# A hand-written order of TensorE's work in two attentions, written out as a string

## The chip, the core and the metric

The kernel runs on one core of one Trainium2 chip. The metric is the time of one execution on the device in microseconds; three runs of the kernel before gave 2184.05, 2185.17 and 2186.51 us, a median of 2185.17 us. The engines of the core work side by side and each takes its own instructions in order: TensorE (PE in the profile; its weight loads are PEld), VectorE (DVE), ScalarE (ACT), GpSimd (POOL), and SyncE (SP), which issues transfers.

## What is computed

The program is a stack of eight blocks on an input of 2 x 512 rows of 512 numbers in fp32: four attentions, each followed by a feed-forward block, each with a layer norm before it and a residual sum after it. The change touches the first attention and the last one. Both have 32 heads and short head vectors:

```python
def L0_attn_a(x, ...):                       # first attention; 4 numbers per head
    C_q = x @ Wq_d + bq_d
    C_kv = x @ Wkv_d + bkv_d
    q = (C_q @ W_qk + b_qk).reshape(b, s, NUM_HEADS, KV_LAT)
    scores = einsum('bqhd,bkd->bhqk', q, C_kv) / sqrt(KV_LAT)
    attn = softmax(scores, axis=-1)          # no mask
    V = (C_kv @ Wv_u + bv_u).reshape(b, s, NUM_HEADS, HEAD_DIM)
    return einsum('bhqk,bkhd->bqhd', attn, V).reshape(b, s, -1) @ Wo + bo

def L1_attn_b(hidden_states, ...):           # last attention; 16 numbers per head
    q, k, v = split(hidden_states @ qkv_w + qkv_b, 3, axis=-1)
    q, k = _rope(q, cos, sin), _rope(k, cos, sin)
    scores = einsum('bqhd,bkhd->bhqk', q, k) * scale
    scores = scores + (1.0 - causal) * MASK_VAL
    probs = softmax(scores, axis=-1)
    ctx = einsum('bhqk,bkhd->bqhd', probs, v).reshape(b, s, e)
    return ctx @ out_w + out_b
```

The two feed-forward blocks and the two attentions in the middle (`attn_gqa`, `attn_mla`) are not touched.

## The kernel before

The heads are worked in quartets. The four heads of a quartet lie in the four groups of 32 rows (partitions) that TensorE's array can use independently, g = 0 to 3. The first attention (`attn_latent_small`) has 16 quartets in one sequence, 8 for each of the two halves of the batch. The last one (`attn_mha`) runs its function `core` once for each half, with 8 quartets in each. Its `core` is compiled in two versions and a register chooses; the causal one is the one that the profile shows running. There the widths of the products differ: a block of 128 queries sees only the keys up to it, so a product is 128, 256, 384 or 512 wide, while in the first attention all are 512 wide.

A quartet u goes through these steps, each a small function that both attentions define and that a common function orders:

- `score(u, j, g)`: one product on TensorE (S in what follows): the scores of block j of 128 queries, head g, into one bank of PSUM (L474, L1263). VectorE reduces the bank to one maximum per row (L482; L1273, which adds the mask first) and writes it into the tile `nm`. There are 16 of these in a quartet, j = 0 to 3 and g = 0 to 3.
- `maxima(u)`: four transposes on TensorE of `nm` (M; L490, L1287), and on VectorE one addition that puts the negative maxima into a spare row of the queries, the tile `qm` (L492, L1289).
- `transposed(u, j, g)`: one product on TensorE (T) of keys with `qm`, so that the scores come out transposed and with the maximum subtracted (L505, L1299), and its exponential on ScalarE (L508, L1309). There are 16 in a quartet. In the last attention GpSimd clears half a block after each four of them (L1313).
- `values(u)`: 16 products of values with the exponentials, all into one bank (L516, L1324). In the first attention VectorE adds that bank to `raw` (L528; ScalarE copies it for each fourth quartet, L526), in the last one ScalarE copies it (L1332).
- `after`: a list of later steps. `divide` transposes `raw` and divides by the sums (L538 to L546 for each fourth quartet of the first attention, L1338 to L1342 for each quartet of the last). In the first attention `flatten` and `project` follow (L559 to L575). `extra` is a list of 11 pieces of the first attention that prepare the second half of the batch (layer norms, latents, queries, values).

Each step that takes a PSUM bank takes the next of eight in a fixed circle: `turn()` (L131) walks through the list `BANKS` of L127. So a product can start only when the engine that reads the bank taken eight turns before has done so.

TensorE's order is written by hand: `manual_schedule(engines={PE})` (L577, L1349) keeps TensorE's instructions in the order in which the program emits them, while a scheduler places those of the other engines. `run_quartets` (L318) emits them. It is one quartet ahead with the scores: in the pass for u it interleaves the 16 scores of u + 1 with the 16 transposed products of u, block by block: for block 0 four scores and then four transposed products, for the others one and one. After each block there is room for one piece of `extra` or `after`. Then `values(u)` follows, and then `maxima(u + 1)`:

```python
            if 0 <= u < n:
                values(u)
                due.append((u, 0))
            if u + 1 < n:
                maxima(u + 1)
```

So the first pass, u = -1, has nothing but 16 scores and the maxima, and the last one has transposed products and no scores.

Of the kernel before, what the change touches and what calls it, by code (L numbers as in the profile page):

```python
# [37 lines left out]
B, S, D = 2, 512, 512  # L38
P = 128
NT = S // P  # L40
# [5 lines left out]
class Block:  # L46
# [268 lines left out]
                )  # L315

    @staticmethod
    def run_quartets(n, score, maxima, transposed, values, after, extra=()):  # L318

        due, extra = [], list(extra)
        for u in range(-1, n + 1):
            pieces = [due.pop(0)] if due else []
            for j in range(NT):
                for m, (kind, g) in enumerate(
                    ((0, 0), (1, 1), (0, 2), (1, 3), (0, 1), (1, 0), (0, 3), (1, 2))
                    if j
                    else ((0, 0), (0, 1), (0, 2), (0, 3), (1, 0), (1, 1), (1, 2), (1, 3))  # L330
                ):
                    if kind == 0 and u + 1 < n:
                        score(u + 1, j, g)
                    if kind == 1 and 0 <= u < n:
                        transposed(u, j, g)
                if extra and u >= 0:
                    extra.pop(0)()
                elif pieces and j < 3:
                    of, done = pieces[0]
                    if done < len(after):  # L340
                        after[done](of)
                        pieces[0] = (of, done + 1)
            for of, done in pieces:
                for f in after[done:]:
                    f(of)
            if 0 <= u < n:
                values(u)
                due.append((u, 0))
            if u + 1 < n:
                maxima(u + 1)  # L350


def attn_latent_small(k, a):
# [8 lines left out]
    with ExitStack() as ctx:  # L362
# [18 lines left out]
        for i in range(2):  # L381
            m = one([P, NT, P], f"nm{i}")
# [82 lines left out]
        extra = prepare(1) + [fold, fold_bias]  # L465

        quartets = [(b, half, i) for b in range(B) for half in range(2) for i in range(4)]
# [107 lines left out]
                k.add_to_x(b * NT + t, ps)  # L575

        with tc.manual_schedule(engines={mybir.EngineType.PE}):  # L577
            k.run_quartets(
                len(quartets), score, maxima, transposed, values, [divide, flatten, project], extra
            )  # L580


def ffn_lora(k, a):
# [569 lines left out]
def attn_mha(k, a, exact):  # L1153
# [5 lines left out]
    T = 4  # L1159
# [3 lines left out]
    with ExitStack() as ctx:  # L1163
# [26 lines left out]
        for i in range(2):  # L1190
            m = one([P, NT, P], f"nm{i}")
# [50 lines left out]
        def core(b, causal):  # L1242
# [17 lines left out]
            def score(u, qt, g):  # L1260
                kv = (qt + 1) * P if causal else S
                ps = k.turn()
                nc.tensor.matmul(  # L1263
                    ps[:, :kv],
                    q[rows[g], u, bass.ts(qt, P)],
                    kk[rows[g], u, :kv],
                    start=True,
                    stop=True,
                )
                at = 32 * g + spare  # L1270
                lo = S - (qt + 1) * P
                mask = k.mask if causal else add
                nc.vector.tensor_tensor_reduce(  # L1273
                    out=ps[:, :kv],
                    in0=ps[:, :kv],
                    in1=mask[:, lo : lo + kv],
                    op0=ALU.add,
                    op1=ALU.max,
                    scale=1.0,
                    scalar=-3e38,  # L1280
                    accum_out=nm[u % 2][:, qt, at : at + 1],
                )

            def maxima(u):
                tp = k.turn()
                for qt in range(NT):
                    nc.tensor.transpose(tp[:, bass.ts(qt, P)], nm[u % 2][:, qt], k.ident)  # L1287
                t = lp.tile([P, S], F32, tag="qm", name="qm")
                nc.vector.tensor_tensor(t, tp, q[:, u], ALU.add)  # L1289
                qm[u] = t  # L1290

            def transposed(u, kc, g):
                if (u, kc) not in probs:
                    pt = lp.tile([P, 4, S], F32, tag="pT", name="pt") if kc % 2 else k.other()
                    probs[u, kc] = [pt, 0]
                pt = probs[u, kc][0]
                lo = kc * P if causal else 0
                ps = k.turn()
                nc.tensor.matmul(  # L1299
                    ps[:, lo:],  # L1300
                    kk[rows[g], u, bass.ts(kc, P)],
                    qm[u][rows[g], lo:],
                    start=True,
                    stop=True,
                )
                if not causal:
                    at = S - P - kc * P
                    nc.vector.tensor_tensor(ps, ps, addT[:, at : at + S], ALU.add)
                nc.scalar.activation(pt[:, g, lo:], ps[:, lo:], AF.Exp, scale=scale)  # L1309
                probs[u, kc][1] += 1  # L1310
                if causal and probs[u, kc][1] == 4:
                    diag = pt[:, :, lo : lo + P]
                    nc.gpsimd.affine_select(  # L1313
                        out=diag, in_=diag, compare_op=ALU.is_ge, fill=0.0, base=0,
                        pattern=[[0, 4], [1, P]], channel_multiplier=-1,
                    )
# [30 lines left out]
                )  # L1347

            with tc.manual_schedule(engines={mybir.EngineType.PE}):  # L1349
                k.run_quartets(8, score, maxima, transposed, values, [divide])  # L1350
            ctxT = k.other()
            for c in range(T):
                tp = k.turn()
# [11 lines left out]
        for b in range(B):  # L1365
            prepare(b)
            with tc.If(exact != 0) as branch:
                core(b, True)
            with branch.Else():
                core(b, False)  # L1370


@with_exitstack
def kernel(ctx: ExitStack, tc: tile.TileContext, a: dict, out: bass.AP):
    k = Block(ctx, tc, a["x"], out)
    attn_latent_small(k, a)
    ffn_lora(k, a)
    attn_gqa(k, a)
    ffn_lora(k, a)
    attn_mla(k, a)  # L1380
    exact = causal_exact(k, a)
    ffn_moe(k, a)
    attn_mha(k, a, exact)
    ffn_moe(k, a, last=True)
# [157 lines left out]
```

## Time and profile before

| what | us | where it is from |
|---|---|---|
| median of three runs | 2185.17 | the times |
| the profiled execution, its own time | 2187.9 | the times |
| span of the profiled execution | 2186.2 | head of the page |
| TensorE busy in the span | 2083.8 | page, part 1 |
| VectorE busy in the span | 1298.2 | page, part 1 |
| quartets of the first attention, first score reduction to last sum | 260 (28.1 to 288.3) | timeline of VectorE |
| one quartet there, undisturbed | 14.0 to 14.1 | starts of L528 and L492 |
| quartets of the last attention, first half | 100.5 (1851.3 to 1951.8) | timeline of TensorE |
| the same, second half | 99.6 (2009.2 to 2108.8) | timeline of TensorE |
| one quartet there | 11.49 | starts of L1289 |

The time of an execution is 1.7 us above its span: work outside the recorded instructions. The profile writes `out<-in` with the program's names of tiles; `sc`, `pj`, `tp` and `av` are PSUM banks. An fp32 product shows as two matrix multiplications, one pass after the other. Several rows of TensorE overlap where they use different groups of rows, so its "busy" share is not a share of its full speed. In a timeline the bracket at the end of a line is the idle time of that engine ahead of the line and what ended it.

### The profile page before, as it was taken

Reading aid. Unit: us, or ns where it says so; the run is one execution under the profiler, and the core shown is the slowest. Engines: PE = TensorE matmul, PEld = TensorE weight load, DVE = VectorE, ACT = ScalarE, POOL = GpSimd, SP = SyncE. Lnnn points to the kernel's source line nnn. Section 1 sums busy time; section 2 is a strip of 40 time slices with the busy share of each in tenths; the row PEclk is TensorE's granted clock in tenths of the full one; section 3 lists DMA queues with packets and bytes.
Section 4 is the critical chain, followed back from the end, with each engine's and each line's share of the span. In section 5 each row is a group of like instructions: output and inputs, shape, how many; then the busy total and the mean of one; then the engine's idle time right before and its main releaser. Section 6 shows DMA issues by size and latency. Waiting matters only on the chain. (4 is left out here: it accounts for less than half of the span.)

```text
span 2186.2 us, 38883 instructions
## 1 busy us (share of the span) xinstructions
PE 2083.8 (95%) x15128; PEld 1094.9 (50%) x15128; DVE 1298.2 (59%) x3478; ACT 731.3 (33%) x2040; POOL 708.8 (32%) x945
## 2 busy tenths in 40 slices
PE   7999989999999999999998989999999889999988
PEld 3444444555555555555554444454544444554545
DVE  6678842655555555555555556666666584755745
ACT  2555621322222222222222155444544111541531
POOL 1100020423322222232322256555555436115211
PEclk9999989999999999999999999999999999999999
DMA  3000021112121212111010322010101102002001
GB/s 96 15 1 1 20 92 58 49 40 68 25 64 25 64 33 65 37 61 49 21 30 6 119 59 71 2 63 10 58 11 50 39 30 43 1 2 39 1 2 39
DMA packets 65751, 85.35 MB, mean 39 GB/s; under 512 B 13458, under 2 KB 50450, under 8 KB 60948
## 3 DMA queue, kind: packets, MB, share of 16 engines
q1 hardware_dynamic: 64916, 81.70, 12.6%
q8 instruction: 123, 2.02, 0.4%
q10 hardware_dynamic: 640, 1.05, 0.3%
q14 instruction: 72, 0.59, 0.1%
HBM read 58.60 MB, written 2.10 MB: 28 GB/s over the span
## 5 line engine op out<-in xcount | busy, mean ns | idle before, releaser
L239 ACT ACTIVATE room<-room,nmax 128x128 f32<-128x128 f32 (+3 forms) x384 | 211.2, 551 | 505.5 <-DVE nmax L229 504.5
L250 POOL TENSOR_SCALAR room<-room,invs 128x128 f32<-128x128 f32 (+3 forms) x384 | 198.0, 536 | 99.2 <-DVE invs L247 99.2
L677 POOL TENSOR_TENSOR q<-q,t 128x512 f32<-128x512 f32 x64 | 81.9, 1280 | 436.3 <-DVE t L676 436.3
L290 PE MATMUL sc<-turned,vals 32*128 32x128 f32 (+7 forms) x1058 | 190.6, 417 | 0.0
L290 PE MATMUL pj<-turned,vals 32*128 32x256 f32 (+7 forms) x692 | 189.0, 424 | 0.0
L290 PE MATMUL tp<-turned,vals 32*128 32x384 f32 (+7 forms) x676 | 158.8, 430 | 0.0
L218 PE MATMUL sc<-kT,q 128*32 128x256 f32 (+15 forms) x1576 | 145.6, 404 | 11.5 <-DVE invs L247 10.8
L263 DVE STREAM_TRANSPOSE turned<-room 128x1152 f32<-128x1152 f32 x80 | 107.9, 1363 | 73.1 <-POOL room L250 22.2
L290 PEld LDWEIGHTS sc<-turned,vals 32*128 32x128 f32 (+1 forms) x1058 | 126.3, 168 | 8.3 <-issue 5.6
L150 PE MATMUL pj<-room,w 128*128 128x512 f32 x272 | 122.2, 599 | 0.0
L181 POOL TENSOR_TENSOR rstd<-ve,mhalf 128x1 f32<-128x1 f32 x80 | 44.8, 562 | 205.3 <-DVE ve L179 192.4
L290 PEld LDWEIGHTS pj<-turned,vals 32*128 32x128 f32 (+1 forms) x692 | 107.1, 169 | 3.9 <-issue 2.2
L150 PE MATMUL sc<-w,room 128*128 128x512 f32 (+1 forms) x240 | 105.5, 582 | 0.0
L150 PE MATMUL sc<-room,w 128*128 128x512 f32 x232 | 105.2, 596 | 0.0
L290 PE MATMUL av<-turned,vals 32*128 32x256 f32 (+7 forms) x358 | 95.7, 420 | 8.8 <-DVE turned L263 8.8
L150 PE MATMUL sc<-w,ctxT 128*128 128x512 f32 x216 | 100.3, 607 | 2.2 <-ACT ctxT L304 2.2
L218 PE MATMUL tp<-kT,q 128*32 128x288 f32 (+15 forms) x1024 | 93.2, 398 | 2.9 <-POOL q L945 2.0
L290 PEld LDWEIGHTS tp<-turned,vals 32*128 32x128 f32 (+1 forms) x676 | 92.2, 169 | 4.4 <-issue 2.7
L239 ACT ACTIVATE probs<-probs,nmax 128x128 f32<-128x128 f32 (+3 forms) x128 | 71.1, 556 | 67.3 <-DVE nmax L229 66.0
L218 PEld LDWEIGHTS sc<-kT,q 128*32 128x32 f32 x1576 | 63.7, 110 | 58.4 <-issue 17.6
L218 PE MATMUL pj<-kT,q 128*32 128x256 f32 (+4 forms) x992 | 87.4, 386 | 4.9 <-DVE invs L247 4.1
L505 PE MATMUL sc<-qm,keys 32*128 32x512 f32 x200 | 86.8, 637 | 0.8 <-DVE qm L492 0.8
(564 smaller groups left out, 5768.8 us busy)
## 6 DMA issues: line engine op xcount, KB each, us to landing
vals<-v SPq DMA_DIRECT2D x256, 64.0 KB, 2.0
w<-in_b_wq SPq DMA_DIRECT2D x8, 1024.0 KB, 5.3
w<-in_b_wo SPq DMA_DIRECT2D x8, 1024.0 KB, 4.8
w<-in_m_wo SPq DMA_DIRECT2D x8, 1024.0 KB, 6.7
w<-in_f_w SPq DMA_DIRECT2D x4, 1024.0 KB, 4.8
w<-in_m_wqn SPq DMA_DIRECT2D x8, 384.0 KB, 3.1
x<-in_x SPq DMA_DIRECT2D x8, 256.0 KB, 4.6
w<-in_b_wk SPq DMA_DIRECT2D x8, 256.0 KB, 2.8
```

The costliest lines, as they stand in the source:

```text
L150: last = self.nc.tensor.matmul(out, lhsT, rhs, start=(i == 0), stop=(i == len(pairs) - 1))
L181: self.nc.gpsimd.tensor_tensor(r, ve, self.mhalf, ALU.pow)
L218: nc.tensor.matmul(ps[32 * i : 32 * i + 32, a - lo : b - lo], q[:, at : at + 32], keys[:, a:b], start=True, stop=True,)
L239: nc.scalar.activation(row, row, AF.Exp, bias=nmax, scale=-1.0, accum_out=total[:, qt : qt + 1])
L250: self.nc.gpsimd.tensor_scalar(row, row, inv[:, qt : qt + 1], 1.0, ALU.mult, ALU.mult)
L263: self.nc.vector.transpose(out[:, :last], probs[:, :last])
L290: self.nc.tensor.matmul(out[:, :, :n], values(i, j), rhs, start=(j == blocks[0]), stop=(j == stop[i]),)
L505: nc.tensor.matmul(ps, keys[b][rows[g], bass.ts(kc, P)], qm[u][rows[g]], start=True, stop=True)
L677: nc.gpsimd.tensor_tensor(out, out, t2, ALU.add)
```

## The change

`run_quartets` gets two more arguments, `lead` and `order`. The scores are now one list over all quartets. The first `lead` of them are emitted ahead of everything (12 in the first attention, 8 in the last). Then each pass follows a string: S is the next score of the list, whatever its quartet, T the next transposed product of quartet u, M the maxima of u + 1, and a bar a place for one piece of `extra` or `after`. What is left of `after` goes behind the string, and `values(u)` comes last in the pass. The groups of rows are taken in the order 0, 2, 1, 3 by the scores and 1, 3, 0, 2 by the transposed products. With 16 S in each string, a pass begins with 12 (or 8) scores of quartet u + 1 already emitted, and the last 12 (8) of its S belong to quartet u + 2. M stands inside the string, behind the score that completes quartet u + 1, and six S stand at its end, in front of the values.

```diff
-    def run_quartets(n, score, maxima, transposed, values, after, extra=()):
+    def run_quartets(n, lead, order, score, maxima, transposed, values, after, extra=()):
+        scores = iter([(u, j, g) for u in range(n) for j in range(NT) for g in (0, 2, 1, 3)])
         due, extra = [], list(extra)
+        for i in range(lead):
+            score(*next(scores))
         for u in range(-1, n + 1):
-            pieces = [due.pop(0)] if due else []
-            for j in range(NT):
-                for m, (kind, g) in enumerate(
-                    ((0, 0), (1, 1), (0, 2), (1, 3), (0, 1), (1, 0), (0, 3), (1, 2))
-                    if j
-                    else ((0, 0), (0, 1), (0, 2), (0, 3), (1, 0), (1, 1), (1, 2), (1, 3))
-                ):
-                    if kind == 0 and u + 1 < n:
-                        score(u + 1, j, g)
-                    if kind == 1 and 0 <= u < n:
-                        transposed(u, j, g)
-                if extra and u >= 0:
+            left = [(j, g) for j in range(NT) for g in (1, 3, 0, 2)] if 0 <= u < n else []
+            for step in order:
+                if step == "S":
+                    at = next(scores, None)
+                    if at:
+                        score(*at)
+                elif step == "T" and left:
+                    transposed(u, *left.pop(0))
+                elif step == "M" and u + 1 < n:
+                    maxima(u + 1)
+                elif step == "|" and extra and u >= 0:
                     extra.pop(0)()
-                elif pieces and j < 3:
-                    of, done = pieces[0]
-                    if done < len(after):
-                        after[done](of)
-                        pieces[0] = (of, done + 1)
-            for of, done in pieces:
-                for f in after[done:]:
-                    f(of)
+                elif step == "|" and due:
+                    due.pop(0)()
+            for f in due:
+                f()
+            due = []
             if 0 <= u < n:
                 values(u)
-                due.append((u, 0))
-            if u + 1 < n:
-                maxima(u + 1)
+                due = [lambda f=f, u=u: f(u) for f in after]
+        for f in due:
+            f()
...
-            k.run_quartets(
-                len(quartets), score, maxima, transposed, values, [divide, flatten, project], extra
-            )
+            order = "STTST|STSTTSSST|STTTTMTSTSTTT|SSSSSS"
+            steps = score, maxima, transposed, values
+            k.run_quartets(len(quartets), 12, order, *steps, [divide, flatten, project], extra)
...
-                k.run_quartets(8, score, maxima, transposed, values, [divide])
+                order = "STTSTSSTSTTSTSTSTTTTS|TTSTMTSSSSSS"
+                k.run_quartets(8, 8, order, score, maxima, transposed, values, [divide])
```

The numbers of instructions on each engine stay the same. On VectorE and ScalarE the scheduler places them in the order in which TensorE now produces the banks they read.

## The prediction

> **What bounds the kernel now.** I read the page first, then the idle times of the score products by source line, then VectorE's timeline over one undisturbed quartet of each attention, and last TensorE's over the same stretches.
>
> ```profile
> span 2186.2 us, 38883 instructions
> PE 2083.8 (95%) x15128; PEld 1094.9 (50%) x15128; DVE 1298.2 (59%) x3478; ACT 731.3 (33%) x2040; POOL 708.8 (32%) x945
> ```
>
> TensorE looks full, but four products on four groups of rows count as four busy rows at once, so 95% only says that it is seldom empty. What its products wait for is in the answer for line 474 (the scores of the first attention):
>
> ```profile
> its engine sat idle before it (us, times) until:
>   DVE nm L482: 31.0, 98
> ```
>
> 98 times a score stood on its bank until VectorE had reduced the score eight turns before; TensorE's order is fixed, so whatever is behind it stood too. VectorE's timeline of one quartet (start, length, idle ahead in brackets):
>
> ```profile
> 219.14 0.69 DVE L528 TENSOR_TENSOR raw<-tp,raw 128x512 f32<-128x512 f32 x1 [2.43 <-PE tp L516]
> 219.75 0.68 DVE L492 TENSOR_TENSOR qm<-sc,qs 128x512 f32<-128x512 f32 x1
> 220.75 0.69 DVE L482 TENSOR_REDUCE nm<-av 128x1 f32<-128x512 f32 x1 [0.32 <-PE tp L474]
> 221.35 0.68 DVE L482 TENSOR_REDUCE nm<-sc 128x1 f32<-128x512 f32 x1
> ...
> 230.09 0.68 DVE L482 TENSOR_REDUCE nm<-tp 128x1 f32<-128x512 f32 x1
> 233.21 0.69 DVE L528 TENSOR_TENSOR raw<-av,raw 128x512 f32<-128x512 f32 x1 [2.43 <-PE av L516]
> ```
>
> Back to back, VectorE takes 0.60 us for one of these (220.75 to 221.35). A quartet has 18: 10.8 us of 14.07 (219.14 to 233.21). It idles 3.27 us: 2.43 while TensorE does the values, the rest around the maxima and in small gaps. So both engines alternate as the bound: VectorE paces the scores, then starves during the values. The last attention is alike:
>
> ```profile
> 2064.07 0.14 DVE L1273 DVE_READ_ACCUMULATOR2_ANT nm<- 128x1 f32 x1
> 2065.71 0.69 DVE L1289 TENSOR_TENSOR qm<-tp,qs 128x512 f32<-128x512 f32 x1 [1.49 <-PE tp L1287]
> ...
> 2068.22 0.26 DVE L1341 RECIPROCAL inv_all<-sc 128x16 f32<-128x16 f32 x1 [0.81 <-PE sc L1338]
> ```
>
> Its reductions step on by 0.25, 0.38, 0.52 and 0.65 us for 128, 256, 384 and 512 columns, four each: 7.2; the addition 0.62 and the division 0.64 make 8.46 of a period of 11.49.
>
> **What the Trainium skill says.** "TensorE: Matmul & The Clock Gate", Part 3 (Packing small matmuls): products on different row groups run side by side, and products keep program order. The trace agrees on both: four scores start within 0.02 us at 219.59, and all wait behind one that waits. "TensorEngine Tiling (Array Packing)", PSUM Bottleneck: packing speeds TensorE, not the reading of PSUM, which may then bound; here that is the 0.60 per score. The same page, Key Properties: a change of tiling mode drains the array. The trace fits: the values start at 215.43, when the last passes of the products (214.91) have run their 0.43 and some 0.1. "PSUM — Partial Sum Buffer", Terms: eight banks, and one product fills at most one; that is the circle of eight.
>
> **The change, part by part.** No instruction is added or removed and no DMA moves; SP's queue is untouched. GpSimd's clearing instructions keep their order; they were off the path (values waited for them at most some tenths). All cost is in TensorE's order, so I walked one steady quartet of each string by hand. Durations: a 512-wide product holds its row group 0.95 us (two passes of 0.43 and 0.1; 206.49 to 207.43); its bank is readable 1.16 us after its start by VectorE, 1.2 by ScalarE; VectorE 0.60 per score, ScalarE 0.48 per exponential (207.70 to 208.20 and on); M 0.59 (219.00 to 219.59); values 3.57 (215.43 to 219.00).
>
> *First attention, zero at the end of the values.* STTS start at 0 on four row groups, TSTS at 0.95: their banks are those of the last T, of the six scores in front of the values and of the sum, read by then. VectorE does the sum (0.3 to 0.9), idles 0.26, and reduces from 1.16 at full pace. The next products stand on banks: TT at 1.84 (the reduction of the first S, 1.16 to 1.76, frees one), SS at 2.2 and 2.4, STST at 2.7 to 3.6, TTT at 3.7 to 4.2, M when the array has drained, 5.1 to 5.7. Its addition runs 5.96 to 6.56, behind the eighth reduction: no wait is longer for it, since its first user is in the next pass. Then T S T at 5.7 to 6.0; S T T want occupied row groups, 6.65; T S S S at 7.5, S S S at 8.4 to 8.5; drained at 9.4, values to 12.97. VectorE idles 0.3, 0.35 and 0.25 between the thinner scores, finishes the six at 12.3, 0.85 before the next sum. Its idle adds up to 2.0: 10.8 + 2.0 = 12.8 to 13.0. I take 13.0: 1.1 less than 14.07. ScalarE has 7.7 of work and ends its last exponential at 9.3, before the last quarter of the values needs it.
>
> Ramps. Before the first T there are now 28 scores, not 16, so VectorE's additional 12 x 0.60 stand in front; some fill time in which TensorE waited. Following the circle, T's start spreads over 42 to 45 us (39.3 before) and the first values end near 58.5 instead of 55.46, one postponed layer norm allowed for: +2.5 to +3. In exchange the pass before last has 4 scores (about 11.2 us: -2.9), and the last begins with T at once instead of M and its addition (277.30 minus 275.7: -1.6). The 11 extra pieces are TensorE's own work (before, their four long quartets exceed 14.07 by about 26 us with the projection); moved from four to three a pass, I count them at nothing, +-4. Sum: 3 - 13 x 1.1 - 2.9 - 1.6 = -16.
>
> *Last attention.* The same walk with its widths (a product holds its row group 0.95, 0.74, 0.53, 0.32; results arrive 1.16, 0.98, 0.77, 0.55 after the start). The pass begins with the eight wide scores of u + 1; VectorE reduces them from 0.98 to 5.66, waiting 0.37 once; the products in between stand on its banks. The transposes for the division run 5.2 to 5.8 and VectorE's division 5.95 to 6.6; M 6.2 to 6.8, its addition 6.95 to 7.57. The six scores in front of the values are narrow (two 128, four 256 wide), start by 7.1, and cost VectorE 2.0 us, 7.57 to 9.59; values wait for the bank of M, 7.67, and take 2.29 (2074.22 to 2076.51): 9.96. VectorE idles 1.5, 8.46 + 1.5 = 9.96. Taken: 10.0, 1.5 less than 11.49. Ramp: in the first pass the extra scores (two of 128 before the addition) hide under the wait for the maxima, and then VectorE is 2.0 us behind: +0.5. Five steady passes: -7.5. The one before last has eight scores only: -2.4. The last has no M and no wait (1943.98 minus 1942.54): -1.45. Sum -10.9 per half, -22 for two. The projections of the second half (1967.9 to 2009) follow on TensorE without a gap and only move forward.
>
> Total -38. Against the profiled execution, 2187.9 - 38 = 2149.9; it was 2.7 over the median, so 2147 for the median.
>
> **Unknown costs.** The trace shows no stretch of these mixed products without VectorE's pacing for long. If row groups packed ideally, TensorE's share of a quartet would be 8.3 + 3.57 + 0.2 = 12.05: eight rounds of 0.86, one more each for the groups that M and the last S leave unfilled, M, and the values. In the last attention it would be about 9.0 (products 2 x 2.14, values 2.29, two sets of transposes 1.18, drains and occupied groups 1.3, an estimate from the rows above). If each bank came 0.1 later than walked in the five places where the chain passes through one, 13.5 and 10.5. A gain beyond VectorE's 10.8 and 8.46 is excluded, as its work is unchanged. That makes the first attention -9 to -28, the last -16 to -33: ends 2160 and 2124. TensorE's clock is low just after the ramps (passes of 0.84 instead of 0.43 around 1861 to 1868); a longer ramp could keep it low, up to +4 in all.
>
> **Rivals.** (a) Full overlap: VectorE never starves, periods 10.8 and 8.5. Then 13 x 3.27 + 10 x 3.0 + ramps (some 8) is about -80: 2105. For it: six scores are 3.6 us of reductions against 3.57 of values. Against: TensorE's own 12.05. (b) Only one string works, since the other stands on banks as long as before; -16 or -22: 2163 to 2169, and 2174 if the ramp eats more of it. For it: in the first attention eleven T come in the first nineteen steps, and ScalarE's pace holds their banks. (c) Slower: the scores run ahead without shortening a period. The mechanism is head-of-line waiting: six scores in front of the values start only as VectorE frees banks, so they delay the values by up to 6 x 0.60 = 3.6 us, more than the 3.27 of idle that they can fill. It decides from the point where VectorE is still four or more scores behind when the first of the six is due; my walk has it one behind. Then a quartet of the first attention takes 14.4, and with the dearer ramp (+3) the kernel is at +5: 2190. (d) The strings do nothing that counts, because waits only change names: 2185.
>
> **Chances.** Forecast 64% (2135 to 2162), stronger overlap, with (a) at its end, 14% (2095 to 2135), (b) 14% (2162 to 2180), (c) 5%, (d) 3%. Range 2122 to 2167. A measurement of this kernel can tell 0.2%, 4.4 us, from no change: faster 0.92, same 0.03, slower 0.05.
>
> **What would show it.** Right: the starts of L528 and L1289 are 12.2 to 13.5 and 9.6 to 10.5 apart; the idle of VectorE ahead of L528 falls from 2.43 to under 1.2; the first exponential comes near 43 us instead of 42.05; M no longer stands before an idle of the transposed products. Wrong: values that wait for VectorE's banks by more than 1 us, periods above 13.7 or 11.2, or a ramp beyond 5 us.

## The result, and the profile after

The changed kernel takes 2171.97 us (median of 4 runs, 2171.32 to 2172.98), the kernel before, run beside it on the same chip, 2185.84 (2184.05 to 2188.02): a ratio of 0.9937, with a 95% interval of 0.9919 to 0.9954. It is faster by 14 us, where 38 were forecast. The profiled executions differ by 16.5 us of span:

```profile
span 2169.7 us, 38898 instructions
PE 2076.7 (96%) x15128; PEld 1102.2 (51%) x15128; DVE 1298.8 (60%) x3478; ACT 725.5 (33%) x2040; POOL 707.3 (33%) x945
```

The work is the same (VectorE 1298.8 us against 1298.2). What went is waiting. The answer for line 474 of the changed kernel shows that the wait on which the forecast rested fell there:

```profile
its engine sat idle before it (us, times) until:
...
  DVE nm L482: 5.6, 15
```

Before, scores stood on their banks 98 times, 31.0 us in all; now it is 15 times, 5.6 us. But that is one line of four. The same wait ahead of the other products of the first attention fell only from 23.1 to 20.7 us (transposed products 6.8 to 10.8, maxima 6.4 to 9.9, values 9.9 to none). The wait of the transposed products for the addition (L492), 10.0 us before, is gone. The idle time for which the profile shows no releaser ("issue") grew from 53.3 to 67.8 us over the four lines. All idle ahead of them together fell from some 126 to 118 us. These are almost all idle times of the weight loads (PEld), so the measure is rough; but by it most of the waiting that left the scores stands elsewhere now.

The starts of the last step of each quartet tell where the 16.5 us are. In the last attention the last copy of the values (L1332) starts at 2092.3 instead of 2108.9 us and, for the first half, at 1944.5 instead of 1951.9. The sum of the first attention (L528) of the last quartet starts at 291.8 instead of 287.6 us, 4.2 us later, of which 0.2 is a later first reduction. From the first score of a half to its last copy, the last attention takes 89.8 and 90.6 us instead of 100.6 and 99.7: it gained 19.9. The other 0.8 us lies in the blocks between the two attentions, which the change doesn't touch and which took 1560.6 to 1564.0 us over all the runs kept. The loss and the gain are read apart from here on.

**The last attention did what was forecast.** ScalarE's timeline over the second half, its rows for L1332 (start, length, idle ahead in brackets; the exponentials between them are left out):

```profile
2064.76 0.59 ACT L1332 COPY raw<-tp 128x512 f32<-128x512 f32 x1 [2.56 <-PE tp L1324]
...
2074.88 0.59 ACT L1332 COPY raw<-sc 128x512 f32<-128x512 f32 x1 [2.57 <-PE sc L1324]
...
2084.47 0.59 ACT L1332 COPY raw<-sc 128x512 f32<-128x512 f32 x1 [2.04 <-PE sc L1324]
...
2092.32 0.59 ACT L1332 COPY raw<-tp 128x512 f32<-128x512 f32 x1 [1.38 <-PE tp L1324]
```

A steady quartet takes 10.12 us (forecast 10.0, before 11.49), the one before last 9.59, the last 7.85 (before 9.22). In VectorE's timeline of a steady quartet one idle of more than 0.1 us is left, behind the values:

```profile
2035.31 0.57 DVE L1273 CUSTOM_DVE_ANT_0 tp<-tp,mask 128x384 f32<-128x384 f32 x1 [1.45 <-PE sc L1263]
...
2041.25 0.69 DVE L1289 TENSOR_TENSOR qm<-av,qs 128x512 f32<-128x512 f32 x1
...
2043.84 0.14 DVE L1273 DVE_READ_ACCUMULATOR2_ANT nm<- 128x1 f32 x1
2045.43 0.57 DVE L1273 CUSTOM_DVE_ANT_0 sc<-sc,mask 128x384 f32<-128x384 f32 x1 [1.45 <-PE sc L1263]
```

Before, the addition (L1289) stood behind 1.49 us of idle; now VectorE comes to it from other work, and 1.45 us stand ahead of the first score behind the values instead. So the idle at the values is about as long as it was. What went are the idle of 0.81 us ahead of the division, which the prediction's lines show, and one of 0.42 us ahead of a score (L1273 at 2070.52).

**The first attention.** VectorE's timeline of an undisturbed quartet of the changed kernel:

```profile
229.64 0.69 DVE L528 TENSOR_TENSOR raw<-tp,raw 128x512 f32<-128x512 f32 x1 [1.01 <-PE tp L516]
230.66 1.89 DVE L482 TENSOR_REDUCE nm<-sc 128x1 f32<-128x512 f32 x3 [0.33 <-PE sc L474]
...
235.55 0.69 DVE L492 TENSOR_TENSOR qm<-sc,qs 128x512 f32<-128x512 f32 x1
236.64 0.69 DVE L482 TENSOR_REDUCE nm<-sc 128x1 f32<-128x512 f32 x1 [0.40 <-PE sc L474]
237.46 0.69 DVE L482 TENSOR_REDUCE nm<-tp 128x1 f32<-128x512 f32 x1
238.36 0.69 DVE L482 TENSOR_REDUCE nm<-sc 128x1 f32<-128x512 f32 x1 [0.21 <-PE av L474]
...
242.99 0.69 DVE L528 TENSOR_TENSOR raw<-pj,raw 128x512 f32<-128x512 f32 x1 [0.95 <-PE pj L516]
```

It takes 13.35 us (13.39 on the mean of four) where 14.03 were needed, and the idle ahead of L528 fell from 2.43 to about 1.0, as forecast. So the steady quartets gained, and yet the whole attention lost. The next table cuts it at the steps L526 and L528 of all 16 quartets; the kernels of the experiments below stand beside the two, so that each can be read there. The first column is from the first score reduction to the sum of quartet 0; the four columns behind it hold quartets 1 to 5 (where most of the 11 extra pieces are, and the first division), one undisturbed quartet (the mean of four), the pair with the projection, the pair with a division only; then come the last two, and the sum. In the rows, "20 and 12" stands for the products ahead of the maxima and behind them, 19 and 13 in the changed kernel.

| kernel | to quartet 0 | 1 to 5 | undisturbed | projection | division | last two | all |
|---|---|---|---|---|---|---|---|
| before | 27.47 | 86.73 | 14.03 | 34.76 | 28.74 | 25.66 | 259.48 |
| changed | 32.85 | 92.67 | 13.39 | 35.59 | 28.24 | 20.54 | 263.45 |
| bars moved | 31.11 | 88.49 | 13.39 | 32.74 | 27.39 | 20.54 | 253.83 |
| lead 8 | 32.50 | 93.43 | 13.75 | 36.35 | 28.95 | 21.94 | 268.18 |
| 20 and 12, bars as changed | 32.01 | 92.16 | 13.67 | 36.00 | 28.77 | 20.50 | 264.11 |
| 20 and 12, bars moved | 31.47 | 89.58 | 13.67 | 33.41 | 27.91 | 20.50 | 257.55 |
| 20 and 12, four bars | 31.71 | 85.86 | 13.67 | 35.88 | 27.92 | 20.49 | 256.53 |
| bars after 8, 16 and 27 | 32.32 | 88.40 | 13.39 | 35.06 | 27.81 | 20.54 | 257.68 |
| bars moved, four bars | 31.54 | 85.95 | 13.39 | 32.75 | 27.39 | 20.54 | 251.73 |

("All" holds four undisturbed quartets.) How far can a row be trusted? Four runs contain the changed kernel's first attention unaltered: the changed kernel, the one of experiment 1, and two that alter the last attention alone. They took 263.44, 265.13, 263.46 and 265.15 us. The 1.7 us lie in one quartet, that of the projection (22.35 instead of 20.65). Where it is longer, the granted clock of TensorE is 0.5 for 3.4 us there, and the passes of the projection's products are 0.85 us apart instead of 0.43. In the table only the row "20 and 12, four bars" has such a stretch in that pair (196.7 to 200.1 us), so its 35.88 and its sum are not compared. Apart from that, the same code differs by less than 0.2 us.

Quartets 1 to 5 got 5.94 us longer, although five quartets should have saved 5 x 0.64 = 3.2. Something costs 9 us there, and these are the passes with the pieces that the forecast "counted at nothing". A part of the 9 is only moved: with three places in a pass instead of four, these quartets hold eight of the 11 extra pieces instead of seven.

TensorE's timeline of the changed kernel shows one such place. It is the division, which the string puts behind `STTST`, that is behind five products:

```profile
180.51 0.69 PE L474 MATMUL av<-keys,qs 32*128 32x512 f32 x1
180.52 0.69 PE L505 MATMUL sc<-qm,keys 32*128 32x512 f32 x1
180.53 0.69 PE L505 MATMUL pj<-qm,keys 32*128 32x512 f32 x1
180.53 0.69 PE L474 MATMUL tp<-keys,qs 32*128 32x512 f32 x1
...
181.48 1.02 PE L505 MATMUL sc<-qm,keys 32*128 32x512 f32 x2
182.43 0.66 PE L538 MATMUL pj<-ident,raw 128*128 128x128 f32 x4
183.01 0.69 PE L474 MATMUL tp<-keys,qs 32*128 32x512 f32 x1
```

Four products start together on the four row groups. The fifth runs alone from 181.48 to 182.43, 0.95 us with three quarters of the array empty, because the next thing in order is a transpose on the whole array. The Trainium skill's page "TensorEngine Tiling (Array Packing)", Key Properties, says that a change of tiling mode drains the array; the forecast cites that for the values, and this row shows what it costs when the round ahead of it is not full. This was the theory that the experiments set out from: **broken rounds**. The string's three bars stand after 5, 14 and 26 products, with the maxima after 19; before, each piece stood after 8 products, two whole rounds.

### The profile page after: what moved, and what is told of

Same layout as the page of the kernel before. It is cut to its first block, busy times and chain, and to the rows that moved or that the text cites. A ratio compares the mean times of both kernels' runs of the same rounds, so it can differ in the third digit from the quotient of the medians.

```text
span 2169.7 us, 38898 instructions
## 1 busy us (share of the span) xinstructions
PE 2076.7 (96%) x15128; PEld 1102.2 (51%) x15128; DVE 1298.8 (60%) x3478; ACT 725.5 (33%) x2040; POOL 707.3 (33%) x945
## 5 line engine op out<-in xcount | busy, mean ns | idle before, releaser
L218 PE MATMUL sc<-kT,q 128*32 128x256 f32 (+15 forms) x1576 | 145.6, 404 | 11.6 <-DVE invs L247 10.8
L505 PE MATMUL sc<-qm,keys 32*128 32x512 f32 x202 | 94.2, 623 | 0.0
```

Source lines behind the costliest of these rows:

```text
L218: nc.tensor.matmul(ps[32 * i : 32 * i + 32, a - lo : b - lo], q[:, at : at + 32], keys[:, a:b], start=True, stop=True,)
L505: nc.tensor.matmul(ps, keys[b][rows[g], bass.ts(kc, P)], qm[u][rows[g]], start=True, stop=True)
```

## The experiments

All ran beside the kernel before. The ratios are to it, with 95% intervals; where several kernels are compared, the table above carries the comparison, since it isn't touched by the rest of the program.

**1 and 2. One string alone.** The loop of the kernel before is kept beside the new one, and one attention is put back to it:

```diff
-                k.run_quartets(8, 8, order, score, maxima, transposed, values, [divide])
+                k.run_quartets_old(8, score, maxima, transposed, values, [divide])
```

> New string in the first attention only, old order in the last. Reading of the two traces: the first attention lost 4 us and the last one won 21, so this kernel should be 3 to 6 us SLOWER than the kernel before: about 2190, stage of the first attention 264 us (260 before). Rival, that the strings share one cause and the first attention's loss is an artefact of one profile: 5 to 10 us faster, 2176 to 2181.

Measured 2191.02 us, ratio 1.0013 (1.0004 to 1.0022).

```diff
-            k.run_quartets(len(quartets), 12, order, *steps, [divide, flatten, project], extra)
+            k.run_quartets_old(
+                len(quartets), score, maxima, transposed, values, [divide, flatten, project], extra
+            )
```

> Old order in the first attention, new string in the last only. If the whole gain is there: 2185.8 - 20.7 = about 2165, so 7 us faster than the changed kernel, with a period of 10.1 us. Rival, gains spread over both: slower than the changed kernel, 2175 or more.

Measured 2167.29 us, ratio 0.9898 (0.9881 to 0.9914). The whole gain comes from the last attention, and the first one's string alone makes the kernel slower by 1 to 5 us (its first attention takes 265.1 us, with the low clock at the projection; that of the second run, in the old order, 259.3). What was forecast as two gains is a gain and a small loss.

**3. The bars beside the maxima.** The order of the products is that of the changed kernel, but the pieces stand ahead of the maxima, behind them, and ahead of the values, where the array drains anyway:

```diff
-            order = "STTST|STSTTSSST|STTTTMTSTSTTT|SSSSSS"
+            order = "STTSTSTSTTSSSTSTTTT|M|TSTSTTTSSSSSS|"
```

> Changed kernel, order of S, T and M untouched, only the three bars moved: next to M (one on each side) and behind the six last S, where TensorE drains its array anyway. Theory of broken rounds (a full-array piece at a bar that does not follow a multiple of four products leaves a round of four row groups unfilled, about 0.9 us each, in the four passes with extra pieces, some eight such places): 6 to 9 us faster than the changed kernel, 2163 to 2166, with the sum of pass 3 (fourth L528 of the stage) some 8 us earlier. Rival, that the ramp of 12 scores or the spreading of the pieces over a fourth pass costs it: no change beyond 2 us, 2170 to 2174.

Measured 2160.78 us, ratio 0.9871 (0.9855 to 0.9888); the first attention is 9.6 us shorter than with the change (253.83 against 263.45) and 5.7 shorter than before. (The spans differ by 9.1 us, the medians by 11; by the ratios it is 14, with intervals of 4 to each side. The lengths in the traces carry the comparison.) So the loss is in where the pieces stand, not in the order of the products: the undisturbed quartet stays at 13.39. Most of it comes from quartets 1 to 5 (4.2), then from the pair with the projection (2.9) and quartet 0 (1.7).

**4. A shorter lead.** The rival of that was the ramp: 12 more scores ahead of the first transposed product.

```diff
-            k.run_quartets(len(quartets), 12, order, *steps, [divide, flatten, project], extra)
+            k.run_quartets(len(quartets), 8, order, *steps, [divide, flatten, project], extra)
```

> Changed kernel with 8 scores ahead instead of 12 in the first attention. Theory of the ramp (each score ahead costs VectorE 0.60 us before the first exponential and is only partly paid back in the pass before last): the missing 9 us sit there, so 4 to 6 us faster, 2166 to 2168. Theory of broken rounds: only the sized part comes back, 4 x 0.60 = 2.4 less about 1 at the end, and M now waits for the reduction of the S five products ahead of it, up to 0.3 a pass the other way: within 3 us of the changed kernel, 2169 to 2174.

Measured 2175.6 us, ratio 0.9937 (0.9921 to 0.9954); the first attention is 4.7 us longer than in the changed kernel. That is slower than either forecast. Quartet 0 ends 0.35 us earlier, and each undisturbed quartet becomes 0.36 longer: a lead of 8 puts the last reduction right ahead of the maxima, and VectorE idles 0.42 ahead of L492. The lead isn't what costs the first attention its gain.

**5 and 6. Whole rounds for the products too.** With 19 products ahead of the maxima and 13 behind, five and four rounds are needed; with 20 and 12 it would be five and three. One T is moved ahead of M, once with the bars of the changed kernel (first line added) and once with those of experiment 3 (second):

```diff
-            order = "STTST|STSTTSSST|STTTTMTSTSTTT|SSSSSS"
+            order = "STTST|STSTTSSST|STTTTTMTSTSTT|SSSSSS"
...
+            order = "STTSTSTSTTSSSTSTTTTT|M|TSTSTTSSSSSS|"
```

> The changed kernel with one transposed product of the first attention's string moved from behind the maxima to ahead of them, bars as they are: 20 products ahead of the maxima and 12 behind, eight whole rounds of four row groups where there were nine. Theory of broken rounds: the steady quartet falls from 13.41 to 12.5-12.8 us, the first attention gets 5 to 9 us shorter, 2162-2168 us. Rival (VectorE's 10.8 us and the circle of banks set the pass, a broken round is hidden): steady quartet stays at 13.2-13.5, 2170-2174 us.

> The bars next to the maxima, as in the run with moved bars, and 20 products ahead of the maxima, 12 behind: no broken round with or without a piece. Theory of broken rounds: the two effects add, some 8 us from the bars and 5 to 9 from the string, 2151-2160 us, steady quartet 12.5-12.8. Rival (the pass is set by VectorE): as with the moved bars alone, 2158-2165 us.

Measured 2170.87 us (ratio 0.9923, 0.9905 to 0.994) and 2165.29 us (0.9897, 0.988 to 0.9915). Here the theory failed. A round less per quartet saved nothing; the undisturbed quartet became 0.28 us longer, 13.67. VectorE's timeline in the first of the two says why:

```profile
234.20 0.68 DVE L482 TENSOR_REDUCE nm<-pj 128x1 f32<-128x512 f32 x1
235.49 0.69 DVE L492 TENSOR_TENSOR qm<-av,qs 128x512 f32<-128x512 f32 x1 [0.60 <-PE av L490]
```

In the changed kernel the addition follows the last reduction with less than 0.1 us between; here the maxima come a product later and VectorE, with nothing queued, idles 0.60. TensorE's timelines give both sides. The maxima start 5.80 us after the sum of the quartet (228.99 to 234.79), in the changed kernel 5.22 (229.64 to 234.86). From there to the values it is 4.19 us (to 238.98) against 4.42 (to 239.28). So the T ahead of the maxima cost 0.58, and of the round saved behind them, some 0.9 us by the theory, only 0.23 arrived. That a broken round is hidden wherever VectorE still has work queued is the reading that fits this; no run shows it alone.

**7. Whole rounds or the place beside the maxima.** Experiment 3 changed both: no piece breaks a round, and each stands beside a drain. Here the pieces stand in the middle of the string, but after 8 and 16 products and 8 behind the maxima, one to three products later than in the changed kernel:

```diff
-            order = "STTST|STSTTSSST|STTTTMTSTSTTT|SSSSSS"
+            order = "STTSTSTS|TTSSSTST|TTTMTSTSTTTS|SSSSS"
```

> The string with moved bars again, but its three bars stand in the middle of the string after whole rounds of four products (8 and 16 ahead of the maxima, 8 behind), not beside the maxima and the values. If the loss of the changed kernel comes from rounds that a piece breaks, whole rounds are enough: the first attention ends within 3 us of the run with moved bars (283.8), 284-287 us, and the kernel takes 2161-2165 us. If what counts is that a piece stands where TensorE drains anyway and VectorE has reductions queued (beside the maxima and the values), it ends as the changed kernel, 290-293 us, 2169-2173.

Measured 2164.27 us, ratio 0.989 (0.9873 to 0.9906). The first attention takes 257.68 us: these places recover 5.8 of the 9.6 us, and those beside the maxima and the values another 3.8. Quartets 1 to 5 come to the same (88.40 and 88.49). Of the 3.8 us, 2.3 are in the pair with the projection and 1.2 in quartet 0.

The run doesn't separate the two explanations for the 3.8 us, as its third bar is not behind whole rounds. Eight products stand there, but by the two orders of row groups they take the groups 2, 0, 1, 2, 3, 0, 2, 1: group 2 three times, hence three rounds, as at the changed kernel's third bar. (In quartets 1 to 5 the same bar loses nothing against experiment 3, so a broken round alone doesn't settle it either.) TensorE's timeline has the last T running on to 186.75, when the others have ended, and only then the projection's first transpose (L569):

```profile
185.80 1.02 PE L505 MATMUL tp<-qm,keys 32*128 32x512 f32 x2
186.75 0.66 PE L569 MATMUL pj<-ident,flat 128*128 128x128 f32 x4
```

VectorE's timeline shows the other explanation in the same place, the projection's first result (L194) behind three reductions only:

```profile
185.99 0.69 DVE L482 TENSOR_REDUCE nm<-av 128x1 f32<-128x512 f32 x1
186.89 0.69 DVE L482 TENSOR_REDUCE nm<-sc 128x1 f32<-128x512 f32 x1 [0.21 <-PE tp L505]
189.45 0.69 DVE L194 TENSOR_TENSOR x<-tp,x 128x512 f32<-128x512 f32 x1 [1.87 <-PE tp L574]
```

The projection keeps TensorE for some 5 us (four transposes, a copy on ScalarE that it waits for, four products, their starts 0.9 us apart), and VectorE had 1.87 us of that without work. In the changed kernel this idle is 2.77. With the piece ahead of the values, all eight reductions of the scores behind the maxima are queued and TensorE's last round is full, and in experiment 3's timeline the idle is gone:

```profile
188.52 0.68 DVE L482 TENSOR_REDUCE nm<-sc 128x1 f32<-128x512 f32 x1
189.12 0.68 DVE L194 TENSOR_TENSOR x<-tp,x 128x512 f32<-128x512 f32 x1
```

**8. Four pieces in a pass.** The change also went from four places to three, so the 11 pieces reach into a fourth pass (quartet 3 takes 22.03 us in the changed kernel, 14.06 before). A second bar is put ahead of the values:

```diff
-            order = "STTST|STSTTSSST|STTTTMTSTSTTT|SSSSSS"
+            order = "STTSTSTSTTSSSTSTTTT|M|TSTSTTTSSSSSS||"
```

> The string with moved bars and a second bar right ahead of the values, so that four extra pieces go into a pass as before the change, and none is left for a fourth pass. If an extra pass costs through its own steady length: the first attention ends some 5 us earlier than with three bars (283.8), 277-281 us, and the kernel takes 2154-2158 us. If two full-array pieces in a row leave VectorE without work for as long as the fourth pass had cost: 282-285 us, 2159-2163.

Measured 2158.52 us, ratio 0.987 (0.9853 to 0.9886). The first attention takes 251.73 us, 2.1 less than with three bars. VectorE's timeline, its rows for L528:

```profile
83.66 0.69 DVE L528 TENSOR_TENSOR raw<-sc,raw 128x512 f32<-128x512 f32 x1 [4.88 <-PE sc L516]
...
104.72 0.69 DVE L528 TENSOR_TENSOR raw<-sc,raw 128x512 f32<-128x512 f32 x1 [2.91 <-PE sc L516]
...
118.14 0.69 DVE L528 TENSOR_TENSOR raw<-tp,raw 128x512 f32<-128x512 f32 x1 [0.95 <-PE tp L516]
```

Quartet 3 is back at 13.42 (104.72 to 118.14; 20.74 in experiment 3), but quartets 1 and 2 gave most of that back, 2.0 and 2.8 us, and VectorE idles 4.88 and 2.91 us ahead of their sums, where it idled 2.92 and 1.63 with three bars. Only the 4.88 stand behind two pieces in a row; ahead of the 2.91 there is one, since the 11 are then used up. So the result lies between the two forecasts, and a part of what the two quartets gave back is the work of the pieces that moved into them. (The end of the first attention, 279.6 us, lies in the first forecast's range only because its first reduction came 2.0 us earlier in this trace.) The medians of experiments 3 and 8 are not apart by more than their intervals; the 2.1 us are read from the traces.

**9 to 12. The same reasoning on the last attention.** Its string puts the division after 21 products (five rounds and one product) and has 25 products ahead of the maxima. Four kernels moved these. The first has 24 and 8 products with the division ahead of the maxima; the second takes the same together with the first attention's string of experiment 6 and a fourth bar in it, in the middle of the last six scores; the third moves the bar alone ahead of the maxima; the fourth is experiment 8 with the last attention's bar after 16 products. (The cut shows only lines of these two strings; the last kernel also has the first attention's line of experiment 8.)

```diff
-                order = "STTSTSSTSTTSTSTSTTTTS|TTSTMTSSSSSS"
+                order = "STTSTSSTSTTSTSTSTTTTSTTS|MTTSSSSSS"
...
+            order = "STTSTSTSTTSSSTSTTTTT|M|TSTSTTSS|SSSS|"
+                order = "STTSTSSTSTTSTSTSTTTTSTTS|MTTSSSSSS"
...
+                order = "STTSTSSTSTTSTSTSTTTTSTTST|MTSSSSSS"
...
+                order = "STTSTSSTSTTSTSTS|TTTTSTTSTMTSSSSSS"
```

> The changed kernel with the last attention's string alone altered: its divide stands right ahead of the maxima after 24 products, with 8 behind, so eight whole rounds and one drain fewer per quartet (the first attention is untouched). Theory of broken rounds: the steady quartet falls from 10.12 to 9.5-9.9 us, 14 times, 3 to 8 us in all, 2163-2169 us. Rival (the idle 1.45 us ahead of the first reduction behind the values is set by the banks): no change, 10.0-10.2, 2170-2174 us.

> Both strings in whole rounds, and a fourth bar in the first attention, on a whole round among the last scores, so that the extra pieces are done in three passes instead of four. If whole rounds are all that counts, and both parts add: 2143-2155 us. If the fourth piece costs as much in a pass as it saves by leaving the later one: 2147-2157, as the run with whole rounds less 3 to 8. If none of the two string parts works: 2158-2165.

> The changed kernel with the divide's bar of the last attention alone moved, from behind the 21st product to right ahead of the maxima; the order of the products is as in the changed kernel. If the divide beside the maxima is what made the pass longer in the run with whole rounds there (VectorE reads both results before the next maxima, and the scores behind wait for its banks): the steady quartet is 10.9-11.4 us, 2180-2188 us. If the transposed product moved behind the maxima made it longer: 9.9-10.2 us, 2169-2173.

> The run with four bars in the first attention, and in the last attention the divide's bar moved forward from behind the 21st product to behind the 16th, where it breaks no round of four and VectorE has more reductions queued. If a broken round costs only where VectorE has nothing queued, nothing is gained: in the changed kernel VectorE's one idle in this quartet is the 1.45 us behind the values, so the steady quartet stays at 10.05-10.15 us, and the kernel within 3 us of the run with four bars. If a broken round of itself costs TensorE's time on the path, the quartet falls to 9.7-9.95 us, 2 to 5 us in all.

| kernel | us | ratio | undisturbed quartet of the last attention |
|---|---|---|---|
| changed | 2171.97 | 0.9937 (0.9919 to 0.9954) | 10.12 |
| 24 and 8, bar ahead of the maxima | 2187.47 | 0.9996 (0.9986 to 1.0005) | 11.16 to 11.27 |
| the same, with 20 and 12 and four bars in the first attention | 2177.14 | 0.9947 (0.9929 to 0.9964) | 11.16 to 11.27 |
| bar alone ahead of the maxima | 2182.37 | 0.9974 (0.9963 to 0.9984) | 10.74 |
| experiment 8, for the last row | 2158.52 | 0.987 (0.9853 to 0.9886) | 10.12 |
| bar after 16, with experiment 8 | 2168.68 | 0.9906 (0.989 to 0.9923) | 10.78 |

In all four the quartet of the last attention became longer, by 0.62 to 1.15 us. No forecast for the first, the second and the last kernel had that; the third kernel's time lies in the range for an effect of the bar, its quartet just under it. So neither the theory nor the rule of experiment 3 (beside the maxima) carries over. Moving the bar alone costs 0.62 us in a quartet, the T moved behind the maxima another 0.5. VectorE's timeline of the run with the bar after 16 shows the two idles that make up its 0.66:

```profile
2035.11 0.42 DVE L1342 TENSOR_TENSOR ctx<-tp,inv_all 128x256 f32<-128x256 f32 x1
2035.45 0.29 DVE L1273 CUSTOM_DVE_ANT_0 tp<-tp,mask 128x128 f32<-128x128 f32 x1
2035.66 0.14 DVE L1273 DVE_READ_ACCUMULATOR2_ANT nm<- 128x1 f32 x1
2036.18 0.30 DVE L1273 CUSTOM_DVE_ANT_0 tp<-tp,mask 128x128 f32<-128x128 f32 x1 [0.38 <-PE sc L1299]
2036.39 0.14 DVE L1273 DVE_READ_ACCUMULATOR2_ANT nm<- 128x1 f32 x1
2036.80 0.69 DVE L1289 TENSOR_TENSOR qm<-av,qs 128x512 f32<-128x512 f32 x1 [0.26 <-PE av L1287]
```

and TensorE's timeline the score that the first of these waits for, itself waiting:

```profile
2035.02 0.48 PE L1299 MATMUL pj<-qm,ks 32*128 32x128 f32 x2
2035.68 0.34 PE L1263 MATMUL tp<-ks,qs 32*128 32x128 f32 x1 [0.18 <-DVE ctx L1342]
```

The score at 2035.68 takes its bank eight turns behind the division, so it is the division's own, and VectorE reads that (L1342) only after all reductions that were queued ahead of it. The bar's place decides which product stands eight turns behind: with the bar after 16 it is the last score ahead of the maxima, after 21 the second score behind them. With the bar alone ahead of the maxima the score there waits for a reduction in the same way (0.16 us, `DVE nm L1273`), and VectorE idles 0.33 and 0.23 us around it. What all four have in common is shown, two idles of VectorE around the maxima (0.33 and 0.23 us, or 0.38 and 0.26) that the changed kernel hasn't. That the bank of the division causes them is read from the order of the waits in two of the runs; which place would be better than the 21st isn't answered.

The fastest are experiments 8 and 3, 2158.52 and 2160.78 us, which the times don't tell apart (ratios 0.987 and 0.9871). Both keep the changed kernel's last attention and beat both kernels.

## Why the prediction was wrong

The steady quartets were walked rightly: they get shorter in both attentions, and in the first one it is the idle ahead of the sum that shrinks, as forecast. How much of that is due to the further lead, to the place of the maxima or to the order of the row groups was not tested one by one; experiment 4 shows only that a lead of 8 is worse than 12 by 0.36 us a quartet. The forecast of 2147 us fails in the first attention alone, which came out at +4.0 (263.45 against 259.48) instead of -16. By the steps of the prediction:

- **"The 11 extra pieces ... I count them at nothing, +-4": this is the step that failed.** They and the later pieces cost some +13 to +14. The sum: 3.97 measured, less a ramp of 3.6 to 4.1, plus 13 quartets x 0.64, plus 5.1 for the last two, leaves 13.3 to 13.8. The working counted TensorE's own time for a piece and not what a piece does where it stands. Moving the bars took 9.6 us of it away (experiment 3), and a fourth bar 2.1 more (experiment 8). A move by no more than one to three products took 5.8 (experiment 7). What makes up the difference, a round still broken there or VectorE's short queue, stays open.
- **Steady quartet 13.0: mis-sized, measured 13.39.** The idle left was walked to 2.0, and it is. But the idle of before, 3.27, was read too large. In the answers by windows (length, then busy time of PE, PEld, DVE, ACT and POOL) VectorE is busy for 11.18 of one quartet before, 219.14 to 233.21 us, and for 11.34 of one of the changed kernel, 229.64 to 243.00:

```profile
219.14:233.21 14.07, 14.07 (x101) 6.32 (x101) 11.18 (x19) 8.29 (x16) 0.00 (x0) 1.00 0.01 1
229.64:243.00 13.36, 13.36 (x104) 6.72 (x108) 11.34 (x19) 8.17 (x16) 0.00 (x0) 1.00 0.00 1
```

  The working took 18 x 0.60 = 10.8, but 0.60 is the step from one start to the next when they follow back to back. An operation with idle after it is busy for its full 0.69. In the whole timeline of the changed kernel's quartet six of the 18 operations are such, and 10.8 + 6 x 0.09 = 11.34. So the idle of before was 14.07 - 11.18 = 2.89 us and not 3.27, and there was less to take. Thirteen quartets gained 0.64 instead of 1.1: some 6 us of the missing 20.
- **Ramp +2.5 to +3: somewhat too small.** Quartet 0 took 5.4 us longer, of which 1.7 went with the bars (experiment 3). That leaves 3.6 with three pieces in it, and 4.1 in experiment 8, which has four in it as before. So the sign "a ramp beyond 5 us" was there, but in part from the pieces, and a lead of 8 brought nothing (experiment 4). The start of T that the working has at 39.3 is that of its weights; the product itself starts at 40.11 before and at 42.29 after.
- **The last two quartets, -2.9 and -1.6: right**, -5.1 in all (20.54 against 25.66). The one before last takes 10.37, where 11.2 were walked, and the last 10.18.
- **Last attention, 10.0 a quartet and -22 for two halves: right**, 10.12 and -19.9.
- **TensorE's own 12.05.** The sum behind it, 8.3 + 3.57 + 0.2, holds nine rounds of 0.86 and the maxima; the words beside it (eight rounds and "one more each" for two places) would make ten, and 0.9 us more.
- **Rivals.** The result lies where rival (b) stood, with one string that works (2163 to 2174), but by another mechanism than the one named: the string of the first attention doesn't stand on banks as long as before, 98 such waits became 15. Rival (d), that waits only change names, may have a part in that: this wait fell by 25 us, the idle over all four lines by some 8. Full overlap (a) is excluded by 1.0 and 1.45 us of idle that remain. Head-of-line waiting (c) did not come: no quartet without a piece is longer than before.

## What to carry to other kernels

Where an order is written by hand, price every interruption by its place: what is left running alone ahead of it, and how much work the pacing engine still has queued while the other is occupied. A rearrangement that gained 0.64 us in each of thirteen regular quartets lost some 13 in the places where the stretch is broken, so walk one regular period and also one with each kind of piece. And test a place again in each loop: one that was good in one attention (beside the maxima) cost 0.6 us a quartet in the other. Count rounds by the row groups that the products take, not by their number.

## What the runs showed that was not expected

- A fp32 product of 512 columns on one row group holds TensorE for 0.95 us ahead of a whole-array operation, about the same as four on four groups (181.48 to 182.43, one; 178.08 to 179.05 in the run of experiment 7, four).
- One round less per quartet (experiment 5) made it longer by 0.28 us, not shorter by 0.9, although the profile has TensorE busy for all of such a quartet (13.36 of 13.36 us in the changed kernel).
- VectorE's step is 0.60 us where the next operation follows at once, and an operation is busy for 0.69 where an idle follows it, so each short idle costs 0.09 us more than it shows. With six of them in a quartet that is half a microsecond.
